# A quarter of the first head group's distance multiplies on GpSimd instead of VectorE

## The chip, the cores and the metric

The kernel runs on one core of one Trainium2 chip, in float32. Its engines work side by side, each through its own list of instructions in order: TensorE (PE in the profile; its weight loads are PEld) multiplies matrices, ScalarE (ACT) takes exponentials, VectorE (DVE) and GpSimd (POOL) do elementwise work, and SyncE (SP) here mostly issues DMA transfers. Semaphores make one engine wait for another. The metric is the time of one execution on the device, in microseconds (us); smaller is better. A time quoted for a kernel is a median of several executions, a profile is one execution.

## The reference

One transformer layer: attention with a penalty on distance (ALiBi), a layer norm, a mixture of experts, another layer norm. There are 2 batches of 2048 positions, 256 features, 16 heads of 16 features. Only the attention is touched by the change:

```python
qkv = (x @ Wqkv + bqkv).reshape(B, L, 3, n_heads, head_dim)
q, k, v = (qkv[:, :, 0], qkv[:, :, 1], qkv[:, :, 2])
scores = jnp.einsum('bqhd,bkhd->bhqk', q, k) / math.sqrt(head_dim)
pos = jnp.arange(L)
bias = -jnp.abs(pos[None, :] - pos[:, None]).astype(jnp.float32)
slopes = jnp.asarray(_alibi_slopes(n_heads))
scores = scores + slopes[None, :, None, None] * bias[None, None]
probs = jax.nn.softmax(scores, axis=-1)
out = jnp.einsum('bhqk,bkhd->bqhd', probs, v).reshape(B, L, D)
x = layernorm(x + out @ Wout + bout)
...
x = layernorm(x + mixture_of_experts(x))
```

After the attention, a router picks two of eight experts for each token (one of the eight does nothing), tokens are scattered into a buffer by expert, each of seven experts runs two matrix products over 512 tokens, and the sums are normalised again.

## The kernel before

**Attention by head groups.** The 16 heads are taken in four groups of four (`g` = 0 to 3), for each of two batches (`b`). A unit is one batch and one group, and the units run in the order (0,0), (0,1), (0,2), (0,3), (1,0) and so on; the last three are split. In a unit the 2048 queries are taken in four blocks of 512 (`n`). The penalty on distance is not added to the scores: exp(score + penalty) is taken as exp(score) times exp(penalty), and the second factor comes from a table. In group 0 the slopes are so steep that keys far from a query contribute nothing and are skipped; all keys kept there are of kind "E" and need the table `e_t` of exp(shift - slope x distance), with distances both ways. The other groups use the table only for the 512 keys at the block itself (kind "D"), and factors on the values and on the results for the others (kinds "A" and "B").

**A step of `block` (lines 586 to 616).** The pieces of keys and queries that are left are packed into bins of 512 columns (`bins`), apart for the first two heads of the group (`hp` = 0) and for the second two (`hp` = 1). A step `i` takes bin `i` of both. TensorE writes the scores of a bin, for two heads side by side, into a PSUM tile `s` (line 597; three such buffers). ScalarE writes their exponentials into an SBUF tile `pr` of up to 2 x 512 columns (line 605; six buffers, shared by both `hp`). Then for every piece of kind D or E VectorE multiplies its part of `pr`, in place, by a window of the table (line 610). A piece 384 columns wide is 2 x 384 elements in each partition, and the profile shows it as 128x768. Only two steps later, after the scores of step `i + 2` have been issued, `add_values` lets TensorE multiply `pr` by the values into the accumulator `acc_E` (line 523), taking for each place in the bins first the piece of `hp` = 0, then that of `hp` = 1.

**What else lies around it.** Between steps `pump` sets a part of some other job: projections of queries, keys and values (`project_qk`, `project_v`, lines 260 to 313), the output projection, and `route` (lines 621 to 766). `project_qk` writes `hi` and `lo` on VectorE (lines 272, 273), squares `hi` on GpSimd into `sq` (line 281) and sends both by DMA from SyncE's queue to HBM, from where the keys and queries of later units are read back. In unit (0,0) most of the projections of batch 0 are still under way. GpSimd also builds the values tiles `va` (lines 489 to 504, and 792 for the first unit), adds the output bias to the residual when that has landed (line 209), multiplies the kept tokens (`kept`, line 713) and issues the scatters of tokens by indirect DMA (`xbuf`, line 753, eight for one call of `route`). In unit (1,0) the tokens of batch 0 are being routed.

**What sets the order.** TensorE and ScalarE run in the order written in the source (`manual_schedule`, line 778). For VectorE, GpSimd and SyncE a scheduler puts the instructions of each engine in one order when the program is built; it does not change while it runs. The tables `e` have one buffer (`p_e`), so the next unit's table is loaded only when the last multiply by the present one is done.

Of the kernel before, what the change touches and what calls it, by code (L numbers as in the profile page):

```python
# [17 lines left out]
ALU = mybir.AluOpType  # L18
# [106 lines left out]
def fast_path(  # L125
# [3 lines left out]
    nc = tc.nc  # L129
# [20 lines left out]
    def st_tile(name):  # L150
        return ps_st.tile([P, 2, QB], F32, tag="st", name=name)
# [207 lines left out]
    def pieces(g, hp, n):  # L359

        r = reach(g, hp)
        up = lambda v: -(-v // 16) * 16
        down = lambda v: v // 16 * 16
        found = []
        if g == 0:
            tiles = [4 * n + 1] + [t for t in range(TB) if t != 4 * n + 1]
            for t in tiles:
                q0 = max(0, down(P * t - r - QB * n))
                q1 = min(QB, up(P * t + P + r - QB * n))
                if t == 4 * n + 1:  # L370
                    q0, q1 = 0, QB
                if q0 < q1:
                    found.append(("E", t, q0, q1))
            return found
        for d in range(1, 4 * n + 1):
            q1 = min(QB, up(r - P * (d - 1)))
            if q1 > 0:
                found.append(("B", 4 * n - d, 0, q1))
        partial = [f for f in found if f[3] < QB]
        found = [f for f in found if f[3] == QB]  # L380
        after = []
        for d in range(TB - 4 * n - 4):
            q0 = max(0, down(QB + P * d - r))
            if q0 < QB:
                after.append(("A", 4 * n + 4 + d, q0, QB))
        full_a = [f for f in after if f[2] == 0]
        part_a = [f for f in after if f[2] > 0]
        return found + partial + full_a + part_a + [("D", t, 0, QB) for t in range(4 * n, 4 * n + 4)]

    def bins(found):  # L390

        made, fill = [[]], 0
        for kind, t, q0, q1 in found:
            if fill and (fill == QB or q1 - q0 == QB and kind != "E"):
                made.append([])
                fill = 0
            while q0 < q1:
                if fill == QB:
                    made.append([])
                    fill = 0  # L400
                w = min(q1 - q0, QB - fill)
                made[-1].append((kind, t, q0, q0 + w, fill))
                fill += w
                q0 += w
        return made
# [5 lines left out]
    def later(gen, wait=0):  # L411
        waiting.append([step + wait, gen])

    def pump():
        for w in waiting:
            if w[0] <= step:
                try:
                    wait = next(w[1])
                except StopIteration:
                    waiting.remove(w)  # L420
                    return
                if wait is not None:
                    w[0] = step + wait
                    return
# [7 lines left out]
    def project_out(b, m, n, at_t):  # L432
        ps = st_tile(f"o_{b}_{m}_{n}").rearrange("p a (u e) -> p (a u) e", e=D)
        for u in range(4):
            nc.tensor.matmul(ps[:, u, :], at_t[:, u * P : (u + 1) * P], wo_sb[:, m, :], start=True, stop=True)  # L435
        xs = x_all[:, b * TB + 4 * n : b * TB + 4 * n + 4, 0:D]
        nc.vector.tensor_tensor(xs, ps, xs, ALU.add)
        if m == 1:
            yield from route(b, n)
        yield 0  # L440
# [94 lines left out]
    def block(b, g, n, ks, va, e_t, f_t, q_t):  # L535
        n0 = f"{b}_{g}_{n}"
        found = [pieces(g, hp, n) for hp in range(2)]
        packed = [bins(f) for f in found]
        left = {}
        for hp in range(2):  # L540
            for kind, _, q0, q1 in found[hp]:
                for jj in range(2):
                    key = (kind, 2 * hp + jj)
                    left[key] = left.get(key, 0) + q1 - q0
        accs, sums = {}, []

        def acc(kind):
            if kind not in accs:
                accs[kind] = ps_acc.tile([P, QB], F32, tag="acc", name=f"acc_{n0}_{kind}")
            return accs[kind]  # L550

        def done(kind):
            a = accs.pop(kind)
            if kind in "BA":
                w = p_t.tile([P, QB], F32, tag=f"w{kind}", name=f"w{kind}_{n0}")
                nc.vector.tensor_tensor(w, a, f_t["BA".index(kind)], ALU.mult)  # L556
                sums.append(w)
                return
            r = a
            if sums:  # L560
                if len(sums) == 2:
                    nc.gpsimd.tensor_tensor(sums[0], sums[0], sums[1], ALU.add)  # L562
                r = sums[0]
                nc.vector.tensor_tensor(r, a, r, ALU.add)

            turned = p_t.tile([P, QB // 32, 32], F32, tag="turned", name=f"turned_{n0}")
            nc.vector.transpose(turned.rearrange("p b r -> p (b r)"), r)
            rec = small.tile([P, QB // 32], F32, tag="rec", name=f"rec_{n0}")
            nc.vector.reciprocal(rec, turned[:, :, HD])
            half = g % 2  # L570
            if not half:
                pairs[b, n] = p_pair.tile([P, QB // 32, 2, HD], F32, tag="pair", name=f"pair_{n0}")
            nc.vector.tensor_tensor(
                pairs[b, n][:, :, half, :],
                turned[:, :, 0:HD],
                rec.unsqueeze(2).to_broadcast([P, QB // 32, HD]),
                ALU.mult,
            )
            if half:
                at_t = p_t.tile([P, QB], F32, tag="at", name=f"at_{n0}")  # L580
                nc.vector.transpose(at_t, pairs.pop((b, n)).rearrange("p b h r -> p (b h r)"))
                later(project_out(b, g // 2, n, at_t), 4)

        blk_ = {"left": left, "acc": acc, "accs": accs, "va": va, "begun": set(), "done": done}
        nonlocal step
        for i in range(max(len(p_) for p_ in packed)):
            made = []
            for hp in range(2):
                if i >= len(packed[hp]):
                    continue  # L590
                bin_ = packed[hp][i]
                ps = st_tile(f"s_{n0}_{i}_{hp}")
                w = bin_[-1][4] + bin_[-1][3] - bin_[-1][2]
                for kind, t, q0, q1, c0 in bin_:
                    for jj in range(2):
                        r = slice(64 * jj, 64 * jj + 64)
                        nc.tensor.matmul(  # L597
                            ps[:, jj, c0 : c0 + q1 - q0],
                            ks[hp][r, t * P : (t + 1) * P],
                            q_t[r, hp, q0:q1],  # L600
                            start=True,
                            stop=True,
                        )
                pr = p_pr.tile([P, 2, QB], F32, tag="pr", name=f"pr_{n0}_{i}_{hp}")
                nc.scalar.activation(pr[:, :, 0:w], ps[:, :, 0:w], AF.Exp, scale=1.0 / math.sqrt(HD))  # L605
                for kind, t, q0, q1, c0 in bin_:
                    if kind in "DE":
                        x0 = QB * n + q0 - P * t + E_ZERO
                        pc = pr[:, :, c0 : c0 + q1 - q0]
                        nc.vector.tensor_tensor(pc, pc, e_t[:, 2 * hp : 2 * hp + 2, x0 : x0 + q1 - q0], ALU.mult)  # L610
                made.append((hp, bin_, pr))
            pending.append((blk_, made))
            if len(pending) > 2:
                add_values(pending.pop(0))
            step += 1
            pump()
# [963 lines left out]
```

## Time and profile before

| | us |
|---|---|
| median of 3 executions | 1331.94 (1330.21 to 1332.78) |
| the profiled execution, device time | 1340.09 |
| its span, first to last instruction | 1338.1 |
| TensorE busy in it | 1184.9 (89%) |
| ScalarE busy | 808.8 (60%) |
| VectorE busy | 750.9 (56%) |
| GpSimd busy | 307.5 (23%) |
| line 610 on VectorE, all groups of heads: 382 instructions | 371.8 |
| line 605 on ScalarE: 820 instructions | 762.1 |

The profiled execution took 8.15 us more than the median. Its mean granted TensorE clock was 0.944 of full speed. Busy time is time in which an engine executes; an instruction that has started but cannot go on counts as busy. In the trace unit (0,0) runs from about 36 us, where its first exponential is taken, to about 161 us, and unit (1,0) from about 612 us to about 697 us.

### The profile page before, as it was taken

The numbers are of one execution on the slowest core, as the hardware profiler recorded it, in microseconds if no ns is written. First come the engines' busy times: TensorE is split into PE (matmuls) and PEld (weight loads), VectorE is DVE, ScalarE is ACT, GpSimd is POOL, SyncE is SP. The second block draws the span as 40 slices with busy tenths as digits, with TensorE's granted clock in tenths as the row PEclk, the third lists the DMA queues.
The fourth block names the chain that finished last, engine by engine and source line by source line (L and its number), as shares of the span: only waits on it lengthen the run. The fifth ranks groups of instructions, "written<-read, shape, count | busy, mean of one in ns | idle before, by whom it ended". The sixth has DMA issues, their size and how long they took to land.

```text
span 1338.1 us, 18892 instructions
## 1 busy us (share of the span) xinstructions
PE 1184.9 (89%) x7065; PEld 501.2 (37%) x7065; DVE 750.9 (56%) x1596; ACT 808.8 (60%) x889; POOL 307.5 (23%) x308
## 2 busy tenths in 40 slices
PE   4747899999999899986889999999988889999994
PEld 3424333333232233333543332223333226655553
DVE  3649775545554377768884444446885343203644
ACT  0314568877778677774467999999865851111330
POOL 1113251111111112224232110110334102222243
PEclk9857999999999899998789999999998989999998
DMA  6778772052322633534151041041165302346531
GB/s 233 237 237 275 243 225 65 17 200 96 110 94 99 216 94 105 177 101 166 33 194 57 17 154 33 16 154 33 60 222 182 127 33 68 110 134 241 174 126 50
DMA packets 115332, 174.14 MB, mean 130 GB/s; under 512 B 31008, under 2 KB 62624, under 8 KB 115232
## 3 DMA queue, kind: packets, MB, share of 16 engines
q1 hardware_dynamic: 103712, 151.18, 34.0%
q0 software_dynamic: 5952, 16.49, 3.5%
q10 hardware_dynamic: 5568, 5.18, 1.1%
q8 instruction: 58, 0.95, 0.3%
q14 instruction: 42, 0.34, 0.1%
HBM read 110.08 MB, written 62.73 MB: 129 GB/s over the span
## 4 chain that ended last, share of the span: by engine, by line
PE 65%; DVE 19%; DMA 6%; ACT 4%; issue 3%; SPq 2%; another core or an unknown queue 1%; ACTq 0%; POOL 0%; DVEq 0%
PE s L597 17%; DVE pr L610 12%; PE acc_B L523 8%; PE acc_A L523 8%; PE h L1023 7%; PE y L1042 7%; PE acc_D L523 6%; ACT pr L605 4%; PE qk L268 4%; PE acc_E L523 2%; PE o L435 2%; DMA k<-kd 2%; DMA vd<-vs 2%; PE v L295 1%; SPq L277 1%
## 5 line engine op out<-in xcount | busy, mean ns | idle before, releaser
L605 ACT ACTIVATE pr<-s 128x1024 f32<-128x1024 f32 (+2 forms) x820 | 762.1, 1060 | 316.2 <-PE s L597 281.0
L610 DVE TENSOR_TENSOR pr<-pr,e 128x1024 f32<-128x1024 f32 (+14 forms) x382 | 371.8, 1016 | 156.3 <-ACT pr L605 152.0
L597 PE MATMUL s<-q,k 64*128 64x512 f32 (+13 forms) x1900 | 350.9, 443 | 56.1 <-DMA k<-kd 20.1
L597 PEld LDWEIGHTS s<-q,k 64*128 64x128 f32 x1900 | 162.4, 195 | 394.7 <-ACT pr L605 251.0
L523 PE MATMUL acc_D<-pr,va 128*32 128x512 f32 x768 | 164.4, 636 | 12.0 <-DVE pr L610 11.2
L523 PE MATMUL acc_A<-pr,va 128*32 128x512 f32 (+5 forms) x1136 | 159.1, 578 | 0.0
L523 PE MATMUL acc_B<-pr,va 128*32 128x512 f32 (+4 forms) x1136 | 153.3, 581 | 0.0
L1030 ACT ACTIVATE ht<-h 128x1024 f32<-128x1024 f32 x28 | 28.7, 1023 | 172.3 <-PE h L1023 156.9
L1042 PE MATMUL y<-w,ht 128*128 128x256 f32 x448 | 103.5, 384 | 12.6 <-DVE ye L1045 12.0
L1023 PE MATMUL h<-xet,w 128*128 128x512 f32 x224 | 99.4, 600 | 1.5 <-DVE xet L904 1.5
L523 PE MATMUL acc_E<-pr,va 128*32 128x128 f32 (+14 forms) x760 | 78.5, 433 | 24.6 <-DVE pr L610 24.4
L1042 PEld LDWEIGHTS y<-w,ht 128*128 128x128 f32 x448 | 82.9, 190 | 31.6 <-DVE ye L1045 20.0
L268 PE MATMUL qk<-xb,wqk_sb 128*128 128x512 f32 x128 | 68.2, 664 | 21.8 <-DMA wqk_sb<-in_wkd 11.1
L500 POOL TENSOR_TENSOR va<-vu,fk_sb 128x768 f32<-128x768 f32 (+2 forms) x36 | 38.3, 1064 | 202.9 <-PE acc_D L523 176.8
L753 POOL DMA_INDIRECT xbuf<-x_all,slot x56 | 61.3, 1094 | 93.9 <-DVE top L745 78.8
L281 POOL TENSOR_TENSOR sq<-hi 128x1024 fp32r<-128x1024 f32 x16 | 33.4, 2088 | 193.4 <-DVE hi L272 168.7
L562 POOL TENSOR_TENSOR wB<-wB,wA 128x512 f32<-128x512 f32 x12 | 25.5, 2126 | 203.2 <-DVE wA L556 203.2
L1023 PEld LDWEIGHTS h<-xet,w 128*128 128x128 f32 x224 | 42.9, 193 | 51.8 <-issue 51.0
L1045 DVE SCALAR_TENSOR_TENSOR ye<-y,xe,sums 128x256 f32<-128x256 f32 x28 | 13.5, 483 | 86.0 <-PE y L1042 86.0
L272 DVE TENSOR_SCALAR hi<-qk,bqk_sb 128x512 fp32r<-128x512 f32 x32 | 23.9, 747 | 51.0 <-PE qk L268 38.3
L523 PEld LDWEIGHTS acc_E<-pr,va 128*32 128x32 f32 x760 | 30.1, 124 | 58.5 <-DVE pr L610 26.3
L913 POOL DMA_INDIRECT sums<-abuf,to x28 | 26.8, 957 | 110.0 <-DVE to L907 69.5
(134 smaller groups left out, 844.4 us busy)
## 6 DMA issues: line engine op xcount, KB each, us to landing
k<-kd SPq DMA_DIRECT2D x88, 256.0 KB
e<-in_c_e SPq DMA_DIRECT2D x11, 1920.0 KB
q<-qd SPq DMA_DIRECT2D x64, 256.0 KB
w<-in_w SPq DMA_DIRECT2D x14, 1024.0 KB
kd<-hi SPq DMA_DIRECT2D x32, 256.0 KB
kd<-lo SPq DMA_DIRECT2D x32, 256.0 KB
qd<-hi SPq DMA_DIRECT2D x32, 256.0 KB
qd<-lo SPq DMA_DIRECT2D x32, 256.0 KB
```

Source lines behind the costliest of these rows:

```text
L268: nc.tensor.matmul(ps[:, 0, :], wqk_sb[:, a, c, m * P : (m + 1) * P], xb[:, c, :], start=(c == 0), stop=(c == 1))
L281: nc.gpsimd.tensor_tensor(sq, hf, hf, ALU.mult)
L500: nc.gpsimd.tensor_tensor(va[:, t0:t1, :, 0:HD], v4[:, t0:t1], fb, ALU.mult)
L523: nc.tensor.matmul(blk_["acc"](kind)[32 * j : 32 * j + 32, q0:q1], blk_["va"][:, t, j, :], pr[:, jj, c0 : c0 + q1 - q0], start=key not in ...
L597: nc.tensor.matmul(ps[:, jj, c0 : c0 + q1 - q0], ks[hp][r, t * P : (t + 1) * P], q_t[r, hp, q0:q1], start=True, stop=True,)
L605: nc.scalar.activation(pr[:, :, 0:w], ps[:, :, 0:w], AF.Exp, scale=1.0 / math.sqrt(HD))
L610: nc.vector.tensor_tensor(pc, pc, e_t[:, 2 * hp : 2 * hp + 2, x0 : x0 + q1 - q0], ALU.mult)
L753: nc.gpsimd.indirect_dma_start(out=xbuf_by[4 * k + u], out_offset=bass.IndirectOffsetOnAxis(ap=slot_i[:, k, u : u + 1], axis=0), in_=x_all ...
L913: nc.gpsimd.indirect_dma_start(out=sums[:, s, :], out_offset=None, in_=abuf[:, :], in_offset=bass.IndirectOffsetOnAxis(ap=to[:, s : s + 1] ...
L1023: nc.tensor.matmul(ps[:, a, :], w1_sb[:, c, (2 * f + a) * P : (2 * f + a + 1) * P], xet[:, c, :], start=(c == 0), stop=(c == 1),)
L1030: nc.scalar.activation(ht[:, 2 * f : 2 * f + 2, :], ps, AF.Relu)
L1042: nc.tensor.matmul(ps[:, s, :], ht[:, f, s * P : (s + 1) * P], w2_sb[:, f, :], start=(f == 0), stop=(f == NC - 1))
```

## The change

In head group 0, on odd steps `i`, the multiplies of the bin of the second two heads (`hp` = 1) are written for GpSimd. The multiplies of `hp` = 0, of even steps and of all other groups stay on VectorE. Operands, sizes and results are the same.

```diff
                 nc.scalar.activation(pr[:, :, 0:w], ps[:, :, 0:w], AF.Exp, scale=1.0 / math.sqrt(HD))
+
+                multiplies = nc.gpsimd if g == 0 and hp == 1 and i % 2 else nc.vector
                 for kind, t, q0, q1, c0 in bin_:
                     if kind in "DE":
                         x0 = QB * n + q0 - P * t + E_ZERO
                         pc = pr[:, :, c0 : c0 + q1 - q0]
-                        nc.vector.tensor_tensor(pc, pc, e_t[:, 2 * hp : 2 * hp + 2, x0 : x0 + q1 - q0], ALU.mult)
+                        multiplies.tensor_tensor(pc, pc, e_t[:, 2 * hp : 2 * hp + 2, x0 : x0 + q1 - q0], ALU.mult)
                 made.append((hp, bin_, pr))
```

In the built programs 68 multiplies change their engine, 34 in each batch. By width as the profile shows it, those of one batch are: two of 1024 elements, six of 768, three of 576, one of 384, six of 320, five of 256, two of 128 and nine of 64, together 12,800 elements in each partition. TensorE's and ScalarE's orders are the same in both programs. On GpSimd the 68 are placed among the instructions that were there, and with them VectorE's and SyncE's orders shift a little: two projections' `lo` come before a multiply that is gone, some loads of keys and values for unit (0,2) are issued a few places later, and so on.

## The prediction

> **What bounds the kernel now.** I read the page's busy line first.
>
> ```profile
> PE 1184.9 (89%) x7065; PEld 501.2 (37%) x7065; DVE 750.9 (56%) x1596; ACT 808.8 (60%) x889; POOL 307.5 (23%) x308
> ```
>
> GpSimd (POOL) looks free. But 56% for VectorE (DVE) is a mean over the whole run; the change acts in units (0,0) and (1,0) alone. So the second view is busy time by window: the second half of unit (0,0), then unit (1,0) in three parts (columns: window, length, busy time and count of PE, PEld, DVE, ACT, POOL, granted clock, DMA share, GB/s).
>
> ```profile
> 98.00:161.00 63.00, 51.46 (x467) 26.64 (x467) 54.70 (x82) 30.41 (x34) 18.03 (x9) 0.82 0.78 249
> 612.00:644.00 32.00, 22.89 (x199) 10.92 (x199) 31.37 (x72) 13.53 (x15) 8.70 (x9) 0.87 0.16 56
> 644.00:675.00 31.00, 29.34 (x270) 18.01 (x270) 25.22 (x76) 14.36 (x18) 10.62 (x8) 0.75 0.21 70
> 675.00:697.00 22.00, 19.33 (x160) 9.31 (x160) 19.88 (x52) 13.92 (x16) 4.65 (x6) 0.77 0.57 197
> ```
>
> VectorE is busy 87%, 98%, 81% and 90% here, TensorE 72% to 95%: each waits for the other by turns. From 36 to 98 us VectorE is busy only 34.8 of 62 us; there projections and their transfers lead. Third, TensorE's waits between 612 and 697 us (total, times, longest):
>
> ```profile
> PE acc_E L523 <- DVE pr L610: 17.3, 7, 7.7
> ```
>
> From 98 to 161 us the same line says 7.0 us. So 24.3 us of TensorE time hang on line 610: a real target. The last view, the timeline of both engines, says whether GpSimd can be used for it (start, length, engine, line, operation, shape).
>
> ```profile
> 120.45 1.18 DVE L286 TENSOR_REDUCE n<-nrm 128x2 f32<-128x1024 f32 x1
> 121.37 4.80 POOL L209 TENSOR_TENSOR x_all<-x_all,bo_sb 128x1024 f32<-128x1024 f32 x2 [4.04 <-DMA x_all<-in_x]
> 121.71 2.25 DVE L610 TENSOR_TENSOR pr<-pr,e 128x224 f32<-128x224 f32 x1
> 123.89 2.56 DVE L573 TENSOR_TENSOR pair<-turned,rec 128x256 f32<-128x256 f32 x1
> ...
> 148.32 0.34 DVE L610 TENSOR_TENSOR pr<-pr,e 128x224 f32<-128x224 f32 x1
> ...
> 149.59 0.41 DVE L573 TENSOR_TENSOR pair<-turned,rec 128x256 f32<-128x256 f32 x1
> ...
> 170.21 0.75 DVE L273 SCALAR_TENSOR_TENSOR lo<-qk,bqk_sb,hi 128x512 fp32r<-128x512 f32 x1
> ```
>
> The 224-wide multiply takes 0.34 us alone and 2.25 us while GpSimd adds the bias: it stands until the first of the two adds is done. The 256-wide one then stands through the second.[...] `lo`, which has one of its big inputs in PSUM, takes its usual 0.75 us though GpSimd's `sq` runs from 170.32 us.
>
> [...]
>
> **Removed and added, instruction by instruction.** VectorE's durations free of GpSimd, from the timeline and line 610's rows: 1024 elements 1.22 us, 768 0.95, 576 0.75, 384 0.54, 320 0.48, 256 0.41, 128 0.28, 64 0.21. For the 34 of one batch: 2x1.22 + 6x0.95 + 3x0.75 + 0.54 + 6x0.48 + 5x0.41 + 2x0.28 + 9x0.21 = 18.3 us. GpSimd's nearest rows are two-input multiplies, 256 wide and 768 wide:
>
> ```profile
> L500 POOL TENSOR_TENSOR va<-vu,fk_sb 128x768 f32<-128x768 f32 x1 | 1.5, 1495 | 9.2 <-DMA vu<-vd 9.2
> L500 POOL TENSOR_TENSOR va<-vu,fk_sb 128x256 f32<-128x256 f32 x1 | 0.6, 622 | 1.7 <-PE acc_E L523 1.7
> ```
>
> That is 0.18 us and 1.7 ns for each element; `sq` alone, 1.89 us for 1024, fits. So 1.89, 1.50, 1.17, 0.84, 0.73, 0.62, 0.40, 0.29 for the same widths: 3.8 + 9.0 + 3.5 + 0.8 + 4.4 + 3.1 + 0.8 + 2.6 = 28.0 us. Bounds: 26 if the small ones start faster[...].
>
> **The lock.** Where the two exclude each other, 18.3 us become 28.0: +9.7 us for each batch. What hides it: in batch 0 the five multiplies of block 0 (3.7 us on VectorE, 5.8 on GpSimd) fall before 98 us, where VectorE has room. From 98 to 161 us VectorE idles 8.3 us[...]. I leave +2 us of 7.7. In batch 1 VectorE idles 8.5 of 85 us, most of it after 644 us[...]: +3 of 9.7. Without cover it is +7.7 and +9.7; if the order falls well, nothing.
>
> **The queue.** GpSimd takes its list in order, and a multiply now stands behind whatever was listed ahead. By the built order there are two bad places. First, block 1, step 5 of batch 0 comes behind `va` of the next unit (line 500), which waits for a transfer until 109.7 us, and `sq`, 1.5 + about 1.9 us. The multiply (2.1 us) ends at about 115.5; its exponential is done at 105.9 and TensorE wants it at about 107.7. So TensorE stops some 8 us. But it then meets fewer blocked VectorE multiplies (in the trace the three begun at 110.2, 112.2 and 115.0 us lost 4.6 us to GpSimd), so +3 net; bounds 0 and 8. Second, the eight scatters of routed tokens stand ahead of block 2, step 1 of batch 1.
>
> ```profile
> 660.47 1.26 POOL L753 DMA_INDIRECT xbuf<-x_all,slot  x1 [38.54 <-DVE top L745]
> ...
> 672.23 0.98 POOL L753 DMA_INDIRECT xbuf<-x_all,slot  x1 [0.30 <-issue]
> ```
>
> They wait until VectorE has the slots, 660.5 us, and last 12.7 us, or 10.1 at 0.96 us each with gaps of 0.30. Then come four multiplies (64, 320, 576, 64), 2.5 us. So the bin is ready at 673 to 676 us. TensorE wants it here:
>
> ```profile
> 662.56 1.49 PE L523 MATMUL acc_E<-pr,va 128*32 128x80 f32 x28
> ```
>
> It stops for 10.5 to 13 us; behind it queue the scores of the next steps, with them ScalarE. VectorE uses the pause to catch up, and a later TensorE wait for it at 683 to 686 us shrinks. I take +10; bounds 3 and 15. The `kept` multiply (line 713), now ahead of block 3, step 1, starts at 682.6 us and takes 1.9; its VectorE input comes before that step's other multiplies, so I cost it at nothing (2 us if TensorE is first there). SyncE: the next table waits for the last multiply of the group, now on GpSimd behind the fourth bias add, which waits for its transfer until 156.0 us. It was issued at 158.05; it may be 2 to 3 us later, but its first user runs at 170.97, so I cost that at nothing. The loads for unit (0,2) that moved have over 100 us of room.
>
> **The sum.** Batch 0: 2 + 3; batch 1: 3 + 10. Together +18 us. Against the profiled execution: 1340.1 + 18 = 1358. That one stood 8.15 us over the median of 1331.94, so the median after is 1350.
>
> **The rivals.**
> A: only the lock costs. The pauses at the two queue places are all given back, since VectorE is then ahead. For it: TensorE already waits in both stages. Against: 10 us is over the slack of two steps. +9 us: 1341.
> B: relief wins, the other side. In unit (1,0) VectorE has a backlog of routing from 601 to 644 us, and gets rid of 18.3 us in each batch. If GpSimd's multiplies fall mostly where VectorE waits[...], half of the 24.3 us of TensorE waits go: 1320. It decides if GpSimd's 28.0 us block VectorE for less than 18.3, and the scatters don't stop TensorE. Against it: in the bias adds' case VectorE was blocked nearly throughout.
> C: worse. The lock is uncovered (7.7 + 9.7), the queue costs 15 in full, and the granted clock, already 0.75 to 0.87 in these windows, sinks in the pauses: +33, 1365.
> D: it all comes out even: TensorE-bound stretches hide it, 1332. VectorE's 87% and 98% speak against it.
>
> **How the numbers follow.** The forecast has 0.52, A 0.22, B 0.09, C 0.12, D 0.05. About 0.2%, 2.7 us, is what a measurement of this kernel can tell from no change. Slower: 0.52 + 0.22 + 0.12 = 0.86; same 0.05 (D); faster 0.09 (B). The range 1333 to 1364 takes in A, D, the forecast with the bounds of its terms, and leaves out B and most of C.
>
> **What would show it.** The lock: multiplies of VectorE in the two units longer by GpSimd's durations, and GpSimd's of 768 elements at 1.5 us or more by what they wait. The queue: TensorE's wait for GpSimd's `pr` as a new line, 10 us of it in one piece behind the scatters at some 660 to 675 us, about 8 us in one near 108. Units (0,0) and (1,0) longer by about 5 and 13 us, all others unchanged. I am wrong if VectorE's busy time falls by nearly 36 us with its multiplies at their free durations, or if TensorE's waits in unit (1,0) shrink.

## The result, and the profile after

| | before | after |
|---|---|---|
| median, us | 1332.16 (1330.21 to 1332.78) | 1351.57 (1347.93 to 1351.95) |
| ratio, 95% interval | | 1.0144 [1.0128, 1.016] |
| profiled execution, us (span) | 1340.09 (1338.1) | 1347.93 (1346.0) |

The change costs 19.4 us; 18 were forecast. In the table of experiments below, microseconds are worked out from ratios, times the 1332 of the kernel before; on that scale the change costs 19.2.

The two profiled executions differ by only 7.8 us, because that of before stood 7.9 us above its median and that of after 3.6 below its own. To see where a difference arises, I compare the start of the k-th exponential in two traces (the landmarks, below); ScalarE takes all exponentials in the same order in both programs. After runs 5.2 us late at the end of unit (0,0), then between 0.6 and 5.2 us late, 1.1 at the start of unit (1,0), and 14.9 us late at that unit's end. So in these two executions unit (0,0) costs 5.2 us and unit (1,0) 13.8. Before's profile then loses some 3 us just behind that unit and another 6 near 1050 us, which after's doesn't lose, where nothing was changed.

From the page of after: its busy line, and its costliest groups of lines 612 (line 610 of before) and 523, first with busy time and mean ns of one, then with idle time of the engine just before them.

```profile
PE 1178.9 (88%) x7065; PEld 495.1 (37%) x7065; DVE 738.1 (55%) x1528; ACT 808.3 (60%) x889; POOL 378.2 (28%) x376
...
L612 DVE TENSOR_TENSOR pr<-pr,e 128x1024 f32<-128x1024 f32 (+11 forms) x314 | 348.0, 1147 | 171.7 <-ACT pr L605 171.4
...
L523 PE MATMUL acc_E<-pr,va 128*32 128x128 f32 (+14 forms) x760 | 80.6, 435 | 49.1 <-POOL pr L612 25.7
...
L612 POOL TENSOR_TENSOR pr<-pr,e 128x64 f32<-128x64 f32 (+7 forms) x68 | 75.2, 1132 | 35.5 <-ACT pr L605 35.3
```

The last line but one belongs beside this of before:

```profile
L523 PE MATMUL acc_E<-pr,va 128*32 128x128 f32 (+14 forms) x760 | 78.5, 433 | 24.6 <-DVE pr L610 24.4
```

GpSimd's 68 multiplies take 75.2 us, where the prediction's prices give 2 x 28.0 = 56.0. Most of the difference is not standing still: the prices were too low. GpSimd's timeline of after has this multiply, beside which VectorE runs nothing:

```profile
161.78 1.82 POOL L612 TENSOR_TENSOR pr<-pr,e 128x768 f32<-128x768 f32 x1
```

It had been priced at 1.50. The multiplies that ran undisturbed took 2.35 us at 1024 elements, 1.80 at 768, 1.41 at 576, 1.00 at 384, 0.86 at 320, 0.73 at 256, 0.46 at 128 and 0.32 at 64; with these the 34 of one batch come to 33.3 us and all 68 to 66.5. So some 9 us of the 75.2 are standing still. VectorE kept 314 multiplies and needs 348.0 us; the 371.8 of before less the 36.6 of the 68 that left would be 335.2, so 12.8 us more than before are lost inside them. All of VectorE's busy time falls by 12.8 us (750.9 to 738.1) where 36.6 left, so about 11 more are lost in its other instructions. Busy shares hide this, since a blocked instruction counts as busy. TensorE's idle time ahead of its matmuls by `pr` is 49.1 us, twice the 24.6 of before, and more than half of it now waits for GpSimd.

The same two stretches of the two units (columns as in the prediction: PE, PEld, DVE, ACT, POOL, clock):

```profile
98.00:161.00 63.00, 44.66 (x428) 22.22 (x428) 48.53 (x56) 26.13 (x30) 41.55 (x32) 0.84 0.70 225
...
644.00:675.00 31.00, 19.56 (x170) 11.96 (x170) 23.79 (x69) 10.79 (x12) 14.09 (x17) 0.71 0.14 49
```

TensorE's busy time falls from 51.46 to 44.66 us in the first and from 29.34 to 19.56 in the second, though GpSimd's rises from 18.03 to 41.55 and from 10.62 to 14.09. VectorE was meant to be relieved, and is: it idles. TensorE is the one that pays. Its waits between 612 and 712 us (total, times, longest):

```profile
PE acc_E L523 <- POOL pr L612: 18.1, 7, 8.4
PE acc_E L523 <- DVE pr L612: 14.0, 6, 7.7
```

Before had 17.3 us for VectorE there. Waits for VectorE hardly shrank, and those for GpSimd came on top. Where they lie is seen in TensorE's timeline of after (start, length; in brackets the idle time before and what ended it):

```profile
114.33 1.92 PE L523 MATMUL acc_E<-pr,va 128*32 128x384 f32 x8 [7.65 <-POOL pr L612]
...
625.50 1.92 PE L523 MATMUL acc_E<-pr,va 128*32 128x512 f32 x8 [5.37 <-POOL pr L612]
...
675.01 1.79 PE L523 MATMUL acc_E<-pr,va 128*32 128x32 f32 x16 [8.36 <-POOL pr L612]
...
695.38 0.56 PE L523 MATMUL acc_E<-pr,va 128*32 128x32 f32 x8 [1.79 <-POOL pr L612]
...
696.94 0.58 PE L523 MATMUL acc_E<-pr,va 128*32 128x160 f32 x8 [1.00 <-POOL pr L612]
...
698.48 1.32 PE L523 MATMUL acc_E<-pr,va 128*32 128x288 f32 x8 [0.96 <-POOL pr L612]
```

These lines show four places, the last three being one. What GpSimd did ahead of three of the four (its timeline):

```profile
109.17 1.49 POOL L500 TENSOR_TENSOR va<-vu,fk_sb 128x768 f32<-128x768 f32 x1 [6.16 <-DMA vu<-vd]
110.63 1.89 POOL L281 TENSOR_TENSOR sq<-hi 128x1024 fp32r<-128x1024 f32 x1
112.48 2.48 POOL L612 TENSOR_TENSOR pr<-pr,e 128x768 f32<-128x768 f32 x2
...
663.86 1.13 POOL L755 DMA_INDIRECT xbuf<-x_all,slot  x1 [5.19 <-DVE slot L752]
...
673.64 0.96 POOL L755 DMA_INDIRECT xbuf<-x_all,slot  x1 [0.30 <-issue]
674.62 5.22 POOL L612 TENSOR_TENSOR pr<-pr,e 128x64 f32<-128x64 f32 x6
...
692.62 2.28 POOL L715 TENSOR_TENSOR kept<-x_all,keep_w 128x1024 f32<-128x1024 f32 x1 [5.77 <-DVE keep_w L710]
694.86 6.52 POOL L612 TENSOR_TENSOR pr<-pr,e 128x64 f32<-128x64 f32 x5
```

Read downwards: each multiply starts the moment the instruction ahead of it ends, and one ahead of it had waited for something else, a transfer of `vu`, the routing's slots, the routing's `keep_w`. The multiply inherits these waits, and TensorE inherits them from the multiply. The place at 625.50 us differs in that nothing ahead of it waited: GpSimd was occupied from 608.5 to 623.0 us with eight scatters, `va` and a `kept` of 1.97 us, and then took 2.4 us for the first of two 1024-wide multiplies.

### The profile page after: what moved, and what is told of

It reads as the page before. It is cut to its first block, busy times and chain, and to the rows that moved or that the text cites. A ratio compares the mean times of both kernels' runs of the same rounds, so it can differ in the third digit from the quotient of the medians.

```text
span 1346.0 us, 18897 instructions
## 1 busy us (share of the span) xinstructions
PE 1178.9 (88%) x7065; PEld 495.1 (37%) x7065; DVE 738.1 (55%) x1528; ACT 808.3 (60%) x889; POOL 378.2 (28%) x376
## 4 chain that ended last, share of the span: by engine, by line
PE 62%; DVE 20%; DMA 7%; ACT 4%; POOL 3%; issue 3%; SPq 1%; ACTq 0%; DVEq 0%; POOLq 0%
PE s L597 16%; DVE pr L612 11%; PE acc_B L523 8%; PE acc_A L523 7%; PE h L1025 7%; PE y L1044 7%; PE acc_D L523 5%; ACT pr L605 4%; PE qk L268 3%; PE acc_E L523 2%; PE o L435 2%; DMA vd<-vs 2%; DMA k<-kd 1%; PE v L295 1%; SPq L277 1%
## 5 line engine op out<-in xcount | busy, mean ns | idle before, releaser
L612 DVE TENSOR_TENSOR pr<-pr,e 128x1024 f32<-128x1024 f32 (+11 forms) x314 | 348.0, 1147 | 171.7 <-ACT pr L605 171.4
L597 PE MATMUL s<-q,k 64*128 64x512 f32 (+13 forms) x1900 | 345.9, 437 | 45.1 <-DMA k<-kd 18.7
L597 PEld LDWEIGHTS s<-q,k 64*128 64x128 f32 x1900 | 158.3, 190 | 379.7 <-ACT pr L605 246.2
L1032 ACT ACTIVATE ht<-h 128x1024 f32<-128x1024 f32 x28 | 28.7, 1024 | 172.4 <-PE h L1025 172.4
L523 PE MATMUL acc_E<-pr,va 128*32 128x128 f32 (+14 forms) x760 | 80.6, 435 | 49.1 <-POOL pr L612 25.7
L1044 PE MATMUL y<-w,ht 128*128 128x256 f32 x448 | 103.5, 384 | 12.5 <-DVE ye L1047 12.5
L268 PE MATMUL qk<-xb,wqk_sb 128*128 128x512 f32 x128 | 68.3, 665 | 23.9 <-DMA xb<-in_xt 12.9
L612 POOL TENSOR_TENSOR pr<-pr,e 128x64 f32<-128x64 f32 (+7 forms) x68 | 75.2, 1132 | 35.5 <-ACT pr L605 35.3
```

Of the source, the lines that this page charges most:

```text
L268: nc.tensor.matmul(ps[:, 0, :], wqk_sb[:, a, c, m * P : (m + 1) * P], xb[:, c, :], start=(c == 0), stop=(c == 1))
L523: nc.tensor.matmul(blk_["acc"](kind)[32 * j : 32 * j + 32, q0:q1], blk_["va"][:, t, j, :], pr[:, jj, c0 : c0 + q1 - q0], start=key not in ...
L597: nc.tensor.matmul(ps[:, jj, c0 : c0 + q1 - q0], ks[hp][r, t * P : (t + 1) * P], q_t[r, hp, q0:q1], start=True, stop=True,)
L612: multiplies.tensor_tensor(pc, pc, e_t[:, 2 * hp : 2 * hp + 2, x0 : x0 + q1 - q0], ALU.mult)
L1032: nc.scalar.activation(ht[:, 2 * f : 2 * f + 2, :], ps, AF.Relu)
L1044: nc.tensor.matmul(ps[:, s, :], ht[:, f, s * P : (s + 1) * P], w2_sb[:, f, :], start=(f == 0), stop=(f == NC - 1))
```

## The experiments

All ratios are against the kernel before on the same chip. Three of the runs (E9 to E11) fell to a chip on which that kernel takes 1347.35 us, and the last to one with 1344.41, so ratios are compared, not times.

| | what runs | ratio, 95% interval | us against before |
|---|---|---|---|
| | the change | 1.0144 [1.0128, 1.016] | +19.2 |
| E1 | the change in batch 0 alone | 1.0032 [1.0017, 1.0047] | +4.3 |
| E2 | in batch 1 alone | 1.0123 [1.0101, 1.0144] | +16.4 |
| E3 | not in the step right behind the scatters | 1.0097 [1.0077, 1.0116] | +12.9 |
| E4 | not in the step right behind `va` | 1.0098 [1.0083, 1.0112] | +13.1 |
| E5 | GpSimd only writes | 1.0057 [1.0037, 1.0076] | +7.6 |
| E6 | the 68 multiplies left out | 0.9831 [0.9809, 0.9854] | -22.5 |
| E7 | not in block 2 of batch 1 | 1.0057 [1.0039, 1.0075] | +7.6 |
| E8 | before, with later bias adds | 0.9935 [0.9917, 0.9952] | -8.7 |
| E9 | at neither queue place (E4's step, E7's block) | 1.0031 [1.0016, 1.0045] | +4.1 |
| E10 | as E9, GpSimd only writes | 0.9991 [0.9976, 1.0006] | -1.2 |
| E11 | E8 and E9 together | 0.9993 [0.9976, 1.0011] | -0.9 |
| E12 | E8 once more | 0.9953 [0.9931, 0.9975] | -6.3 |

**E1 and E2: which batch.** One edit each:

```diff
-                multiplies = nc.gpsimd if g == 0 and hp == 1 and i % 2 else nc.vector
+                multiplies = nc.gpsimd if g == 0 and hp == 1 and i % 2 and b == 0 else nc.vector
```

and `b == 1` for the other. Expected of batch 0:

> Only batch 0's 34 multiplies are on GpSimd; batch 1 is as before. In the profile of the changed kernel the end of unit (0,0) is 5.2 us later than before, of which 3.3 to 3.9 us are left at the end of batch 0. Lock and queue together: +3 to +5 us, 1336 +- 2, and nothing of it in unit (1,0). If the extra time came from batch 1 alone: no change.

Of batch 1:

> Only batch 1's 34 multiplies are on GpSimd. If the two units add up: 19.4 less what the batch 0 run costs, +13 to +16 us, 1346 +- 3. If the first unit's delay is what makes the second worse (another alignment with the routing): clearly under +13.

The parts are +4.3 and +16.4; together 20.7, for 19.2 of the whole. So the batches add up within the intervals, and batch 1 holds most of the loss: four fifths by these runs, 13.8 of 19.0 us by the landmarks.

**E3 and E4: each queue place by one step.** The condition has `(b, n, i) != (1, 2, 1)` in E3 and `!= (0, 1, 5)` in E4 added.

> The change, but the one bin (batch 1, block 2, step 1: 4 of the 68 multiplies) that stands behind the eight scatters stays on VectorE. Queue: TensorE's stop of 8.4 us at 666.6 us goes, VectorE gets 1.7 us more: 6 to 9 us faster than the change, 1344 +- 2. Lock alone: 4 of 68 multiplies, half a us, 1351.

> The change, but the one bin (batch 0, block 1, step 5: 2 of the 68) that stands behind the values tile of the next unit stays on VectorE. Queue with the lock: TensorE's stop of 7.65 us near 107 us goes, but then VectorE's multiplies meet GpSimd's va, sq and bias add again, which cost 4.6 us before: 2 to 4 us faster than the change, 1348.5 +- 2. Queue without lock: 7 us faster, 1344. Lock alone: 1351.

E3 gains 6.3 us on the change, at the lower edge of what was expected, because the stop isn't gone but moved. TensorE's timeline in E3:

```profile
687.08 1.92 PE L523 MATMUL acc_E<-pr,va 128*32 128x384 f32 x16 [7.11 <-POOL pr L612]
```

The next odd step's multiplies now stand first behind the scatters. E4 gains 6.1 us, the size that had been put to the queue without a lock, but its trace doesn't bear that out. Its GpSimd timeline:

```profile
109.81 2.87 POOL L281 TENSOR_TENSOR sq<-hi 128x1024 fp32r<-128x1024 f32 x1
112.65 3.31 POOL L209 TENSOR_TENSOR x_all<-x_all,bo_sb 128x1024 f32<-128x1024 f32 x1
115.93 5.11 POOL L612 TENSOR_TENSOR pr<-pr,e 128x128 f32<-128x128 f32 x7
```

With the one step on VectorE, the multiplies of another stand behind `sq` and a bias add, and TensorE stops 6.75 us for them at 116.5 us. The landmarks of E4 show 3.0 us less than the change in unit (0,0) and nothing elsewhere. What the rest of the 6.1 is stays open; the two intervals allow a difference of 3 to 4 us.

**E7: the whole block.** Condition `(b, n) != (1, 2)`: 11 of batch 1's 34 multiplies go back to VectorE.

> The change without the multiplies of block 2 of batch 1, so that none stands behind the scatters. Lock plus queue: TensorE's stop near 666 us doesn't move to a later step but goes, -8 to -11 us against the changed kernel: about 1342, range 1339 to 1345. Lock alone: these are 8 of 34 multiplies of the batch with about a quarter of their time, -2 to -4: 1348. If the loss sits elsewhere in unit (1,0): 1351.

It gains 11.6 us on the change. The stop at the scatters is gone, no wait for GpSimd over 0.8 us is left behind 632 us, and by the landmarks unit (1,0) costs 3.6 us where it cost 13.8. So block 2 is worth about 10 us. That is not the scatters' place alone: the 11 multiplies (the expectation counted 8) also stop locking VectorE out, for which it allowed 2 to 4 us.

**E5: GpSimd occupied, but not reading.** A multiply occupies GpSimd's queue and also reads `pr` and the table. This run takes the reading away and leaves the occupation (the products of these bins are left out):

```diff
-                        multiplies.tensor_tensor(pc, pc, e_t[:, 2 * hp : 2 * hp + 2, x0 : x0 + q1 - q0], ALU.mult)
+                        if multiplies is nc.gpsimd:
+                            for _ in range(1 + (q1 - q0 >= 128) + (q1 - q0 >= 256)):
+                                nc.gpsimd.memset(pc, 1.0)
+                            continue
```

> In place of each of GpSimd's 68 multiplies it fills the same piece one to three times with ones: it occupies its queue at the same places but reads nothing from SBUF; the products of these bins are left out. Lock plus queue (my theory): VectorE's multiplies go back to their free durations and it is relieved of 36 us, but TensorE's stops at the two queue places (7.7 and 8.4 us) stay: about 1343, range 1338 to 1347. Lock alone: no stop of TensorE for GpSimd over 3 us, and the relief wins: 1320 to 1331. Queue alone, without a lock: no change against the changed kernel, 1351, with VectorE's multiplies as before.

It gains 11.6 us on the change, and TensorE still stops: 9.0 us at 115.4, and between 612 and 712 us

```profile
PE acc_E L523 <- POOL pr L614: 16.2, 7, 8.1
PE acc_E L523 <- DVE pr L616: 10.9, 4, 7.7
```

So both mechanisms are there. Where the lock hits is read from the busy time of the multiplies in the two units (busy time by window, that line and engine alone; count in brackets), and from the rest of VectorE's busy time there:

| | 36 to 166 us: VectorE | its other work | GpSimd | 612 to 712 us: VectorE | its other work | GpSimd |
|---|---|---|---|---|---|---|
| before | 62.16 (x95) | 30.6 (x43) | | 66.31 (x99) | 16.8 (x110) | |
| after | 56.82 (x61) | 25.7 (x39) | 38.67 (x34) | 46.75 (x61) | 27.0 (x111) | 36.51 (x34) |
| E5 | 45.27 (x61) | 26.0 (x40) | 31.63 (fills) | 46.34 (x63) | 21.9 (x119) | 31.94 (fills) |

In unit (0,0) VectorE's multiplies lose 11.6 us to GpSimd's reads (56.82 against 45.27): 34 multiplies went away and it is only 5.3 us less busy. In unit (1,0) its multiplies lose almost nothing, but the routing's instructions between them do: about as many take 27.0 us where they took 16.8 in before and 21.9 in E5. One group of four in VectorE's timelines, first of before, then of after:

```profile
641.49 1.37 DVE L638 TENSOR_SCALAR x_all<-x_all,mv,r_ln 128x256 f32<-128x256 f32 x4
...
650.83 3.29 DVE L640 TENSOR_SCALAR x_all<-x_all,mv,r_ln 128x256 f32<-128x256 f32 x4
```

They have one big input. In after the first of the four, ahead of GpSimd's multiplies, takes 0.40 us; the last two take 1.90 and 0.82 us beside GpSimd multiplies of 1.84 and 0.79 us that began up to 0.11 us earlier. What sets them apart from `lo` in the prediction's fence is not shown. GpSimd's own multiplies lose some 5 us in unit (0,0) and 3 in unit (1,0) against the 33.3 that they take undisturbed.

What this costs is another question. By the landmarks E5 is 6.5 us ahead of the change near 155 us, but only 0.5 at the end of unit (0,0), since TensorE waits longer for `k` there (12.4 us for 8.5); unit (1,0) costs 5.6 us in place of 13.8. So nearly all that reaches the end arises in unit (1,0). A part of it may be occupation: the fills hold GpSimd 1.4 to 1.7 us less in each unit than undisturbed multiplies would.

**E6: what relief is worth.** The 68 multiplies are left out (`if multiplies is nc.gpsimd: continue`).

> Leaves the 68 multiplies out altogether (the exponentials of these bins are not multiplied by the table): it prices the relief that the change was after, with neither lock nor queue. TensorE's waits for line 610 are 24.3 us in the two stages, so 24 us is the most; about half of that if the rest turns into waits for ScalarE: 1320, range 1314 to 1327. If VectorE doesn't bound these stages (even out): 1330 to 1334.

It came out at 1309.7 us, 22.5 faster than before, below the range expected. By the landmarks 17.7 us of the gain arise in unit (1,0) and none in unit (0,0), where TensorE's waits for the multiplies fall from 7.0 us to 1.8, but those for `k` and for the norms `n` grow as much (9.6 to 12.5 us, 0.5 to 3.3). In unit (1,0), which lies earlier here, its waits for the multiplies fall from 17.3 us only to 12.1 (600 to 680 us):

```profile
PE acc_E L523 <- DVE pr L614: 12.1, 6, 7.7
```

The rest is TensorE itself. Between the same two exponentials of the unit, behind that long first wait, the windows are these of before, after and E6 (columns as in the prediction):

```profile
617.87:697.68 79.81, 68.39 (x617) 37.11 (x619) 71.28 (x191) 42.49 (x48) 19.93 (x20) 0.82 0.29 100
618.96:712.59 93.63, 68.64 (x615) 35.45 (x615) 67.61 (x158) 42.87 (x49) 54.60 (x54) 0.80 0.23 80
614.56:676.70 62.14, 56.36 (x617) 31.97 (x615) 55.30 (x158) 42.37 (x48) 20.20 (x19) 0.97 0.37 128
```

For the same matmuls TensorE is busy 56.36 us in E6 instead of 68.39, at a granted clock of 0.97 instead of 0.82: 12.0 of the 17.7 us. In the change its busy time is that of before, so its loss there is idle time. So the target was real, in batch 1: leaving the multiplies out brings about 22 us, the most that relief could, and the way it was had is 42 us above that.

**E9 and E10: at neither place, with and without the lock.** E9 joins the conditions of E4 and E7 (55 multiplies stay on GpSimd); E10 has E5's fills in their place.

> The change without its multiplies at both queue places: none in block 2 of batch 1, none at step 5 of block 1 of batch 0; 55 of the 68 stay on GpSimd. Lock plus queue: the two gains add up, -10.1 and -6.6 against the changed kernel: 1335, range 1331 to 1339, a little slower than before or even with it, no stop of TensorE for GpSimd over 6 us. If the queue makes its stop wherever a multiply stands, the -6.6 is not found again: 1340 to 1342. If the relief wins once the stops are gone: below 1330.

> As the run without multiplies at either place, but the 55 that stay on GpSimd only fill their piece (their products are left out): neither lock nor queue, relief alone. Lock: 10 to 14 us less than with multiplies at the same places, about 1322, range 1316 to 1328. No lock: the same time as with multiplies, within 3 us.

E9 at +4.1 is within what the sum of both gains allowed, although two stops for GpSimd are left (6.76 us at 117.4, behind a bias add, and 5.35 at 627.5, behind `kept`), the first longer than expected. E10 missed: 5.3 us less than E9 by the ratios, where 10 to 14 were expected, and not faster than before. My text said that it had neither lock nor queue; its trace still has stops for GpSimd of 7.0, 4.7 and 3.5 us. With the scatters' place gone the reads are worth half as much as in E5. So the two gains don't simply add; why is not shown.

**E8, E11 and E12: the lock used the other way.** In before three VectorE instructions, begun at 115.03, 121.71 and 123.89 us, lost 2.2, 1.9 and 2.1 us beside GpSimd's bias adds (the first, a multiply 160 wide, took 2.48 us, and 0.31 at 145.07 us with GpSimd idle; the prediction's fence has the others). E8 is the kernel before, every multiply on VectorE, with these adds made to wait:

```diff
+    bo_late = const.tile([P, D], F32, name="bo_late")
...
-        nc.gpsimd.tensor_tensor(xs, xs, bo_sb.unsqueeze(1).to_broadcast([P, 4, D]), ALU.add)
+        nc.gpsimd.tensor_tensor(xs, xs, bo_late.unsqueeze(1).to_broadcast([P, 4, D]), ALU.add)
...
+        if u == 0:
+            nc.scalar.copy(bo_late, bo_sb)
```

> The kernel before with all multiplies on VectorE; GpSimd's four bias adds read a copy of the bias that ScalarE makes after unit (0,0), so they run after the stretch in which VectorE is short of time. With a lock: the multiplies[...] go back to their free durations there, -3 us: 1329, range 1326 to 1332. Without a lock, or if the adds lock VectorE out later at the same price: 1332.

1323.41 us, 8.7 faster than before, where 3 were expected and 6 allowed. VectorE's timeline in E8:

```profile
118.61 0.32 DVE L611 TENSOR_TENSOR pr<-pr,e 128x224 f32<-128x224 f32 x1
118.86 0.41 DVE L574 TENSOR_TENSOR pair<-turned,rec 128x256 f32<-128x256 f32 x1
```

These are the two instructions of the prediction's fence, 2.25 and 2.56 us there. TensorE's timeline in E8 behind them:

```profile
120.65 1.49 PE L524 MATMUL acc_E<-pr,va 128*32 128x112 f32 x16
...
123.56 1.06 PE L524 MATMUL acc_E<-pr,va 128*32 128x384 f32 x16 [0.75 <-DVE pr L611]
```

Before had stops of 1.62 and 3.66 us here. By the landmarks E8 is 8.8 us ahead of before at 137 us, and 5.1 at the end of the unit; the adds now run from 147.0 us, in between.

> The later bias adds together with the 55 multiplies on GpSimd. With a lock the multiplies give nothing also where GpSimd is empty: 1323 + 2, range 1322 to 1330. If GpSimd's bias adds were what spoiled the change: below 1320.

> The kernel with the later bias adds alone once more, since the run that combined it with multiplies on GpSimd came out at 0.9993 of the kernel before, on a chip on which that kernel itself takes 15 us longer. If the gain belongs to the kernel: a ratio of 0.992 to 0.995 again, and the 55 multiplies cost 7 us even without the bias adds. If it belongs to the chip: 0.998 to 1.001, and the multiplies cost nothing there.

E12 repeats the gain on another chip, 0.9953 [0.9931, 0.9975]. E11, with the 55 multiplies in addition, is at 0.9993 on a third: 1331 us on the scale of 1332, just outside its range. Taken together the multiplies cost some 0.4% there, 5 us, also without the bias adds, but the two ratios come from different chips and their intervals touch. The fastest whole kernel of this study is the one with later bias adds and no multiply on GpSimd.

## Why the prediction was right, by its steps

**Bound and target.** TensorE and VectorE wait for each other by turns in the two units: right. E6 gets 22.5 us by leaving the multiplies out, close to the 24.3 us of TensorE's waits that were called the target, but that is luck: these waits fell by only 5.2 us in each unit, and 12.0 of the 17.7 us in unit (1,0) are matmuls at a higher granted clock, for which the forecast had no term. Rival B priced half of the 24.3. The relief was undervalued, and it didn't matter, since it never arrived.

**The lock.** Seen in both directions: VectorE's multiplies of unit (0,0) take 56.82 us beside GpSimd's multiplies and 45.27 beside its fills (E5), and GpSimd's 34 multiplies take 38.67 and 36.51 us in the two units for 33.3 undisturbed. How much of it would stay uncovered, +2 and +3 us, was my estimate. Some work did keep its time in before: `hi` took 0.74 us at 60.19 us beside `sq` (0.75 at 140.14 with GpSimd idle), a reduction 1.22 at 78.12 beside another `sq` (1.21 at 154.50), a transpose 0.72 at 160.43 beside `va` (0.70 at 119.81). The working counted the 34 multiplies as 28.0 us on GpSimd against 18.3 on VectorE, and the 28.0 was too low: undisturbed the multiplies take 33.3. Its prices came from the rows of `va`, whose second operand is a broadcast, and of `sq`, which multiplies `hi` by itself; whether that is why they run faster (1.50 us for 1.80 at 768 elements, 1.89 for 2.35 at 1024) was not tested. So the ratio of GpSimd's time to VectorE's at 768 elements is 1.90 (1.80 to 0.95 us), where the prediction's prices have 1.58 (1.50 to 0.95). In batch 1 the lock also acted elsewhere than thought, on the routing's instructions (27.0 us for 16.8). The nearest measure of the terms is E5 against the change, by the landmarks: 0.5 us in unit (0,0) for +2, and 8.2 in unit (1,0) for +3. The lock was priced too high in one and too low in the other.

**The queue.** Both places are where they were put. Behind `va` and `sq` TensorE stopped 7.65 us, "some 8" in the forecast; unit (0,0) costs 5.2 us by the landmarks and 4.3 by E1, for 2 + 3. Behind the scatters it stopped 8.36 us for a forecast of 10.5 to 13: the scatters waited for the slots until 663.9 us as TensorE, too, was some 4 us later by then. The term of +10 is supported in size (E7: 11.6 us by the ratios, 10.2 by the landmarks), but E7 takes the lock of 11 multiplies away as well; E3, which excuses the first step alone, gains 6.3. E3 shows what the forecast hadn't: most of the wait is handed to the next multiply (7.11 us for 8.36).

**What was costed at nothing.** `kept` ahead of block 3: this step failed. The forecast had its VectorE input come early enough; in after `keep_w` came at 692.6 us, TensorE was there at 693.6, before `kept` had ended, and it waited 1.79 + 1.00 + 0.96 = 3.75 us for the multiplies behind it, of which two also ran longer than undisturbed (1.60 us for 0.86, 1.58 for 1.41). The first `kept`, ahead of unit (1,0)'s first odd step, wasn't seen at all: a stop of 5.37 us. With 8.36 at the scatters and some small ones TensorE's stops for GpSimd make 18.1 us; its waits for VectorE fall from 17.3 to 14.0. Together that is +14.8 for a unit that costs 13.8. So the forecast's 3 + 10 came out right as a sum while its parts did not: two stops costed at nothing, a shorter one at the scatters and fewer waits for VectorE cancel. That is luck. The loads of tables and of unit (0,2) on SyncE's queue cost nothing that the landmarks show, as forecast: after is 5.2 us late at the end of unit (0,0) and 1.1 at the start of unit (1,0).

**The rivals.** A, the lock alone with queue stops given back, falls: with GpSimd only writing (E5) TensorE's stops stay (9.0 and 8.1 us) and the kernel is still slower than before. B, relief, falls for this way of getting it. D falls with the result. C's full 15 us at the queue and its sinking clock were not needed: the clock was 0.71 in the stretch of the scatters, where before has 0.75, but over unit (1,0) TensorE is busy 68.6 us for 68.4 before.

## What to carry to other kernels

Before elementwise work goes from VectorE to a GpSimd that looks idle, read GpSimd's list: every instruction ahead of the moved one brings its own waits along. Here the first scatter had waited 5.19 us for its slots and TensorE stopped 8.36 us for the multiplies behind the scatters, and with the one step that stood there taken back it stopped 7.11 us for the next (E3). Price the moved instruction by one with the same kind of operands: here borrowed rows gave 28.0 us for 33.3. Don't count on the two engines working side by side: here VectorE was rid of 36.6 us of multiplies and its busy time, in which standing still counts as work, fell by 12.8. And look at what GpSimd already runs where VectorE is late: with its bias adds put off, the kernel was 8.7 and 6.3 us faster (E8, E12).

## What the runs showed that had not been expected

TensorE's own speed is not the same throughout. In unit (1,0) eight matmuls of nearly the same widths took 1.05 us in before, behind a stop of 2.47,

```profile
623.07 1.05 PE L523 MATMUL acc_E<-pr,va 128*32 128x512 f32 x8 [2.47 <-DVE pr L610]
```

and 1.92 in after, behind the stop of 5.37 at 625.50 us shown above. The granted clock is 1.00 in the first stretch and 0.50 in the second. The length of the last stop alone doesn't decide it here: in before such matmuls took 1.93 us at 116.51 us, with a clock of 0.50, soon after a stop of only 2.29. What decides it is not shown.

The forecast had no term for this. In the change it didn't need one, since over unit (1,0) TensorE's busy time is that of before (68.64 and 68.39 us); in E6 it is most of the gain there (12.0 of 17.7 us). It may also be a part of why E8 brought more than the 3 us that its stalls alone were taken to be worth: from 98 to 161 us the granted clock is 0.89 there and 0.82 in before. No run here separates that.
